# Two layers of adaptive-norm attention and feed-forward blocks on one core: exponentials straight from PSUM in the first attention, a PSUM bank of its own for the sums of squares in local attention, and empty places in the output stages

## The chip, the core and the metric

The kernel runs on one core of one Trainium2 chip, in one launch. The metric is the device time of one execution in microseconds (us). The engines are named as the profile names them: PE is TensorE (PEld its weight loads), DVE is VectorE, ACT is ScalarE, POOL is GpSimd and SP is SyncE, which issues the DMAs. Each engine works through its own instructions in order, and a semaphore holds an instruction back until what it needs is there.

## What is computed

The reference takes x of shape (2, 2048, 128) and runs two outer layers, all in float32. Cut to what matters:

```python
def layer(x, c, wmod, attention, model):
    sa, ca, ga, sb, cb, gb = modulation(c, wmod)       # per batch, 128 wide
    x = x + ga * attention(norm(x) * (1 + ca) + sa)
    x = x + gb * model(norm(x) * (1 + cb) + sb)
    return x

# L0 attention: 16 heads of 8; inside chunks of 64 positions a causal softmax,
#   across chunks a fast-weight state that is updated chunk by chunk (64 updates)
# L0 model: depth 6, 16 heads of 64, window 32;  L1 model: depth 2, 8 heads of 64, window 64
# L1 attention: causal linear attention (elu features) with its own feed-forward block

for l in range(depth):                                 # both models
    q, k, v = split(shift(x) @ Wqkv[l])
    q, k = rotary(l2norm(q) * qs, l2norm(k) * ks)      # l2norm: a root over 64 numbers
    p = softmax(mask(q @ k_window.T * 8))              # own and previous window
    x = x + (p @ v_window) @ Wo[l]
    a, g = split(layernorm(shift(x)) @ W1[l] + b1)
    x = x + (a * gelu(g)) @ W2[l] + b2
```

## The kernel before, in words

**First attention** (`l0_attention`). After the projections it walks over 32 tiles of 128 positions (`order`, `NT = 32`), under an order written out by hand (`manual_schedule`: every engine gets its instructions in the order in which the program makes them). Tile `i` passes through `spread` (POOL), `scores` (PE, into `ps_s`, two PSUM banks), `shifted` (DVE takes the row maximum of 16 groups of 64, line L430, and subtracts it, L432; ACT then makes one exponential over 1024 elements in SBUF, L433), `weights` (DVE sums, L438, and inverts, L439; POOL multiplies, L440), `keys_first` (PE transposes, L448; ACT copies out, L452), `values` (PE, L458; ACT copies to `vbd`, L465) and `mix` (64 small matmuls, L477; ACT copies to `hT`, L484). One turn of the loop works on four tiles at once: `keys_first(i)`, `weights(i+1)`, `scores(i+2)`, `values(i+1)`, `shifted(i+2)`, `mix(i)`.

Between these parts are seven places per tile, `slot(i, 0)` to `slot(i, 6)`, into which the items of the list `todo` are dealt out by the count `due`. Items 0 to 63 are `step(t)`: the 64 updates that form the products of transitions, four DVE instructions each (L374, L375, L377, L379). Item 64 writes them out (`products_done`). The other 65 items are the second part of the same attention: `transitions`, 32 `chain(n)` items, and `out_`, `centre`, `variance`, `scale` for each block of 512. `chain(n)` multiplies the running state by a transition (PE into `ps_n`, L560), adds the new write by a matmul with the identity (L565), copies the sum to SBUF (DVE, L571), and multiplies the old state with the output weights (PE, L575; ACT copies out, L580). The 64 updates are spread over the first 26 tiles, the rest over the last six.

**Local attention** (`local_models`). Eight layers (six of 16 heads, two of 8) of 32 tiles each make 256 rounds. Here a scheduler orders each engine's instructions by its own estimate of times, and picks which free buffer a PSUM tile gets. A round `i` holds, in the program: `scores(i+1)` (two PSUM banks from `psA`, L996 and L1005; DVE takes the maximum, L1013, and subtracts, L1015), ACT's exponential (L1022), DVE's sum (L1029) and inverse (L1030), POOL's product (L1031); `project(i+3, u)`, twice where there are 16 heads; `keys_first_(i)` (`ps_pT`, L1040; ACT copies, L1041); `mix(i)` (`ps_o`, L1058; ACT copies, L1064); `values(i+2)` (`ps_v`, L965; ACT copies, L966, and DMAs spread the rows); `turn(i+2)` (`ps_turn`, L946; ACT copies, L949 and L951) and `project_out(i)` (`ps_y`, L1075; DVE adds, L1081).

`project` is the part that the change touches. PE writes 1024 columns into a wide PSUM tile `ps_qk` (L879). ACT squares them (L881), DVE makes two products with the rotary table (L891, L896), POOL adds these (L902). After the last of the tile's projections DVE sums the squares of each head (L907) and takes a reciprocal root in nine small instructions (`rsqrt_quick`, L173 to L186), whose result `rq_y` POOL multiplies on (L914). The sums and the root's intermediate values lie in the last `ps_qk` itself:

```python
nc.vector.tensor_reduce(
    pq[:, 16 * v:16 * v + 16],
    st[i].pop(("sq", v)).rearrange("p (h d) -> p h d", d=DH), AX.X, ALU.add,
)
y = rsqrt_quick([pq[:, k * 32:k * 32 + 2 * H] for k in range(4)], 2 * H, wk)
```

The eight PSUM banks are shared out as `psA`, two wide tiles of two banks (`ps_qk`, `ps_s`), and `psT`, four single banks for all the others (`ps_pT`, `ps_o`, `ps_v`, `ps_turn`, `ps_y`, and `ps_c`, `ps_r`, `ps_f`, `ps_fy` of the feed-forward part).

The feed-forward part of a block of 512 positions is cut into seven items (`centre`, `variance`, `rest`, `scale`, `gate`, `up`, `down`) of which `step()` takes one at two places of each round. What follows a model (the linear attention after the first, `output` after the second) is cut in the same way, and `lstep()` takes one item at six places of each round. `output(b, k)` has three items: `fetch` loads a block of x, `residual` adds the model's result on DVE (L1205), `leave` transposes it on PE (L1449), copies it (ACT, L1453) and stores it. `rest` is an item that does nothing.

Of the kernel before, what the change touches and what calls it, by code (L numbers as in the profile page):

```python
# [72 lines left out]
def tile_kernel(ctx: ExitStack, tc: tile.TileContext, a: dict, out: bass.AP):  # L73
    nc = tc.nc
    DRAM = bass.MemoryType.DRAM
    PSUM = bass.MemoryType.PSUM
# [35 lines left out]
    identb = const.tile([128, 128], BF16, name="identb")  # L112
# [81 lines left out]
    def l0_attention():  # L194
# [18 lines left out]
        maskb = cp.tile([128, 8, 64], BF16, name="maskb")  # L213
# [8 lines left out]
        m, m1 = modulation()  # L222
# [185 lines left out]
        def scores(i):  # L408
            t0 = 128 * order[i]
            kx = L[i].pop("kx")  # L410
            sp = L[i]["s"] = psS.tile([128, 1024], F32, name="ps_s")
            for q in range(2):
                nc.tensor.matmul(
                    sp[:, 512 * q:512 * q + 512], lhsT=identb,
                    rhs=maskb.rearrange("p h k -> p (h k)"), start=True, stop=False,
                )
            for c in range(2):
                for q in range(2):
                    nc.tensor.matmul(
                        sp[64 * c:64 * c + 64, 512 * q:512 * q + 512],  # L420
                        lhsT=qT[64 * q:64 * q + 64, t0 + 64 * c:t0 + 64 * c + 64],
                        rhs=kx[64 * q:64 * q + 64, c].rearrange("p h j -> p (h j)"),
                        start=False, stop=True,
                    )

        def shifted(i):

            v = L[i].pop("s").rearrange("p (q h k) -> p h q k", q=2, h=8)
            mx = wk.tile([128, 8, 2], F32, name="mx")
            nc.vector.tensor_reduce(mx, v, AX.X, ALU.max)  # L430
            sm = L[i]["p"] = wk.tile([128, 8, 2, 64], F32, name="sm", bufs=3)
            nc.vector.tensor_tensor(sm, v, bc(mx.unsqueeze(3), (128, 8, 2, 64)), ALU.subtract)  # L432
            nc.scalar.activation(sm, sm, AF.Exp)  # L433

        def weights(i):
            sm = L[i]["p"]
            rs = wk.tile([128, 8, 2], F32, name="rs")
            nc.vector.tensor_reduce(rs, sm, AX.X, ALU.add)  # L438
            nc.vector.reciprocal(rs, rs)  # L439
            nc.gpsimd.tensor_tensor(sm, sm, bc(rs.unsqueeze(3), (128, 8, 2, 64)), ALU.mult)  # L440

# [109 lines left out]
        def chain(n):  # L551
            c = n % 8
            pm = E["p"][:, :, 128 * (n % 2):128 * (n % 2) + 128].rearrange(
                "p q (b f) -> p q b f", b=2)
            px = E["p"][:, :, 256:512].rearrange("p q (b f) -> p q b f", b=2)
            if n < 31:
                for b in range(B):
                    for q in range(2):
                        if n:
                            nc.tensor.matmul(  # L560
                                pm[QS[q], q, b], lhsT=E["bd"][QS[q], b, c],
                                rhs=E["m"][QS[q], b], start=True, stop=False,
                            )
                    for q in range(2):
                        nc.tensor.matmul(  # L565
                            pm[QS[q], q, b], lhsT=ident[QS[q], QS[q]],
                            rhs=E["rm"][QS[q], c % 2, b, c // 2], start=(n == 0), stop=True,
                        )
                mn = wk.tile([128, 2, 64], F32, name="mn")
                for q in range(2):  # L570
                    nc.vector.tensor_copy(mn[QS[q]], pm[QS[q], q])  # L571
            if n:
                for b in range(B):
                    for q in range(2):
                        nc.tensor.matmul(  # L575
                            px[QS[q], q, b], lhsT=E["m"][QS[q], b], rhs=wo10[QS[q], :],
                            start=True, stop=True,
                        )
# [93 lines left out]
        def slot(i, part):  # L672

            nonlocal done
            if i < 0:
                return
            q = 7 * i + part + 1
            due = 5 * q // 14 if i < 26 else 65 + (len(todo) - 65) * (q - 182) // 42
            while done < due:
                todo[done]()  # L680
                done += 1

        for i in range(-3, NT):
# [12 lines left out]
            slot(i, 2)  # L696
            if 0 <= i + 2 < NT:
                shifted(i + 2)
            slot(i, 3)
            if i >= 0:  # L700
                mix(i, 0)
                slot(i, 4)
                mix(i, 1)
            slot(i, 5)
            slot(i, 6)
            if i == -1:
                regroup()
# [8 lines left out]
    def local_models(mA, mB, hs0):  # L716
# [153 lines left out]
        def project(i, u):  # L870
            g, b, t = tiles[i]
            m, _ = layers[g]
            H, units = m.H, m.units
            tb = tabs[g, t]
            hw = hs[0][:, b, t * 128:(t + 1) * 128]
            pq = wide("qk")
            for j in range(2):
                js = slice(512 * j, 512 * j + 512)
                nc.tensor.matmul(pq[:, js], lhsT=hw, rhs=wts[g, u][:, js], start=True, stop=True)  # L879
            sq = wk.tile([128, 1024], F32, name="sq", bufs=2)  # L880
            nc.scalar.activation(sq, pq, AF.Square)  # L881
            r = wk.tile(
                [128, 1024], F32, tag=f"r{u if len(units) == 2 else i % 2}", name="r", bufs=2
            )
            t2 = wk.tile([128, 1024], F32, name="t2", bufs=1)
            same = units[u][0][0] == units[u][1][0]
            for e in range(1) if same else range(2):
                s = units[u][e][0]
                hn = 16 if same else 8
                es = slice(512 * e, 512 * e + 64 * hn)  # L890
                nc.vector.tensor_tensor(  # L891
                    r[:, es].rearrange("p (h d) -> p h d", d=DH),
                    pq[:, es].rearrange("p (h d) -> p h d", d=DH),
                    bc(tb[:, 0, s].unsqueeze(1), (128, hn, DH)), ALU.mult,
                )
                nc.vector.tensor_tensor(  # L896
                    t2[:, es].rearrange("p (h s d) -> p h s d", s=2, d=32),
                    pq[:, es].rearrange("p (h s d) -> p h s d", s=2, d=32)[:, :, ::-1, :],
                    bc(tb[:, 1, s].rearrange("p (s d) -> p s d", s=2).unsqueeze(1),
                       (128, hn, 2, 32)), ALU.mult,  # L900
                )
            nc.gpsimd.tensor_tensor(r, r, t2, ALU.add)  # L902
# [531 lines left out]
        def output(b, k):  # L1434
# [181 lines left out]
```

## Time and profile before

The time before is 4924.19 us, the median of three runs (4922.71 to 4925.23). The profiled execution took 4920.01 us; its span from the first to the last instruction is 4918.2 us, so 1.8 us lie around it.

| engine | busy us | share of the span | instructions |
|---|---|---|---|
| PE | 4474.6 | 91% | 73028 |
| PEld | 3055.6 | 62% | 73058 |
| DVE | 3946.2 | 80% | 6822 |
| ACT | 2635.7 | 54% | 4206 |
| POOL | 2780.6 | 57% | 1666 |

The shares are means over stages that are limited by different things, so the stages are read one by one. On the time axis of the span, the first part of the first attention with its 64 updates runs from 97 to 377 us, its second part with the chain to 546 us; local attention begins at 560 us, the linear attention is woven in around 3950 to 4350 us, and the blocks of the output leave between 4620 us and the end. In rows of the profile, "idle before" is the time for which an engine stood still ahead of an instruction, and the name behind `<-` is what ended that time. A busy PE is not a PE at its peak: matmuls are pipelined and their ends are modelled.

### The profile page before, as it was taken

The numbers are of one execution on the slowest core, as the hardware profiler recorded it, in microseconds if no ns is written. First come the engines' busy times: TensorE is split into PE (matmuls) and PEld (weight loads), VectorE is DVE, ScalarE is ACT, GpSimd is POOL, SyncE is SP. The second block draws the span as 40 slices with busy tenths as digits, with TensorE's granted clock in tenths as the row PEclk, the third lists the DMA queues.
The fourth block names the chain that finished last, engine by engine and source line by source line (L and its number), as shares of the span: only waits on it lengthen the run. The fifth ranks groups of instructions, "written<-read, shape, count | busy, mean of one in ns | idle before, by whom it ended". The sixth has DMA issues, their size and how long they took to land.

```text
span 4918.2 us, 166304 instructions
## 1 busy us (share of the span) xinstructions
PE 4474.6 (91%) x73028; PEld 3055.6 (62%) x73058; DVE 3946.2 (80%) x6822; ACT 2635.7 (54%) x4206; POOL 2780.6 (57%) x1666
## 2 busy tenths in 40 slices
PE   5657799999999999999999999999999998899997
PEld 4445566666666666666666666666666665556554
DVE  6993488888888888888887888888877777788886
ACT  3323355555555556555555555556555555465554
POOL 3332376666666666666665666666655544455552
PEclk8778899999999999999999999999999999999999
DMA  2000222222222322222222322222222111111121
GB/s 78 1 1 25 86 69 68 64 73 73 70 67 62 83 68 68 65 75 72 69 65 63 80 71 70 64 77 67 65 52 58 52 49 48 35 46 49 51 58 42
DMA packets 222467, 295.31 MB, mean 60 GB/s; under 512 B 75656, under 2 KB 95408, under 8 KB 221744
## 3 DMA queue, kind: packets, MB, share of 16 engines
q1 hardware_dynamic: 221744, 284.67, 22.0%
q8 instruction: 576, 9.44, 0.8%
q14 instruction: 147, 1.20, 0.1%
HBM read 40.98 MB, written 10.75 MB: 11 GB/s over the span
## 4 chain that ended last, share of the span: by engine, by line
PE 47%; DVE 26%; ACT 7%; POOL 5%; issue 4%; DMA 1%; SPq 0%; POOLq 0%; DVEq 0%; ACTq 0%
PE ps_qk L879 11%; PE ps_o L1058 5%; DVE ps_qk L907 5%; DVE t L896 5%; PE ps_f L1158 5%; PE ps_v L965 5%; PE ps_turn L946 4%; POOL r L902 4%; PE ps_y L1075 4%; DVE r L891 3%; PE ps_s L1005 3%; PE ps_fy L1183 3%; ACT sq L881 2%; DVE rs L1029 2%; PE ps_pT L1040 2%
## 5 line engine op out<-in xcount | busy, mean ns | idle before, releaser
L902 POOL TENSOR_TENSOR r<-r,t 128x1024 f32<-128x1024 f32 x448 | 1059.6, 2365 | 905.5 <-DVE t L896 800.1
L914 POOL TENSOR_TENSOR r<-r,rq_y 128x1024 f32<-128x1024 f32 x448 | 843.9, 1902 | 520.5 <-DVE rq_y L186 497.5
L881 ACT ACTIVATE sq<-ps_qk 128x1024 f32<-128x1024 f32 x448 | 460.4, 1028 | 1077.0 <-PE ps_qk L879 1010.5
L879 PE MATMUL ps_qk<-wp,hs 128*128 128x512 f32 x1792 | 885.7, 616 | 114.4 <-DVE rq_y L186 85.4
L891 DVE TENSOR_TENSOR r<-ps_qk,tb 128x1024 f32<-128x1024 f32 (+1 forms) x512 | 550.3, 1075 | 202.3 <-ACT sq L881 188.9
L896 DVE TENSOR_TENSOR t<-ps_qk,tb 128x1024 f32<-128x1024 f32 (+1 forms) x512 | 554.1, 1082 | 147.7 <-POOL r L902 147.1
L1058 PEld LDWEIGHTS ps_o<-pT,v 64*64 64x64 f32 (+1 forms) x26624 | 479.0, 135 | 304.7 <-ACT pT L1041 162.0
L1031 POOL TENSOR_TENSOR sm<-sm,rs 128x1024 f32<-128x1024 f32 x256 | 487.6, 1905 | 210.7 <-DVE rs L1030 124.3
L1058 PE MATMUL ps_o<-pT,v 64*64 64x32 f32 (+1 forms) x26624 | 529.7, 221 | 35.6 <-ACT pT L1041 18.9
L907 DVE TENSOR_REDUCE ps_qk<-sq 128x16 f32<-128x1024 f32 x448 | 549.0, 1225 | 11.9
L879 PEld LDWEIGHTS ps_qk<-wp,hs 128*128 128x128 f32 x1792 | 308.6, 192 | 370.4 <-issue 233.8
L946 PEld LDWEIGHTS ps_turn<-ident,r 128*128 128x128 f32 x3584 | 409.0, 142 | 125.9 <-issue 98.6
L965 PE MATMUL ps_v<-wp,hs 128*128 128x512 f32 x896 | 482.5, 639 | 1.5 <-ACT oT L1064 0.8
L1075 PEld LDWEIGHTS ps_y<-oT,wo 128*128 128x128 f32 x3584 | 430.3, 193 | 46.5 <-issue 42.4
L946 PE MATMUL ps_turn<-ident,r 128*128 128x128 f32 x3584 | 445.1, 276 | 11.2 <-POOL r L914 5.2
L1075 PE MATMUL ps_y<-oT,wo 128*128 128x128 f32 x3584 | 446.2, 277 | 1.5 <-ACT oT L1064 1.5
L1064 ACT COPY oT<-ps_o 128x512 f32<-128x512 f32 x448 | 243.4, 588 | 282.8 <-PE ps_o L1058 282.1
L1013 DVE TENSOR_REDUCE mx<-ps_s 128x16 f32<-128x1024 f32 (+1 forms) x256 | 312.5, 1221 | 95.9 <-PE ps_s L1005 94.1
L1005 PE MATMUL ps_s<-kT,qT 64*32 64x64 f32 (+1 forms) x26624 | 377.2, 230 | 0.1
L1005 PEld LDWEIGHTS ps_s<-kT,qT 64*32 64x32 f32 (+1 forms) x26624 | 325.6, 107 | 62.6 <-issue 51.7
L1158 PE MATMUL ps_f<-fx,w 128*128 128x512 f32 (+1 forms) x768 | 356.0, 600 | 2.5 <-DVE fx L1141 1.7
L1029 DVE TENSOR_REDUCE rs<-sm 128x16 f32<-128x1024 f32 (+1 forms) x256 | 310.5, 1213 | 51.1 <-ACT sm L1022 49.0
(265 smaller groups left out, 6833.2 us busy)
## 6 DMA issues: line engine op xcount, KB each, us to landing
v<-vn SPq DMA_DIRECT2D x1276, 128.0 KB
v<-vn SPq DMA_DIRECT2D x744, 64.0 KB
v<-vn SPq DMA_DIRECT2D x64, 256.0 KB
wp<-in_L_ffn_Wqkv SPq DMA_DIRECT2D x20, 512.0 KB
xD<-xb SPq DMA_DIRECT2D x24, 256.0 KB
xb<-xD SPq DMA_DIRECT2D x24, 256.0 KB
cs<-in_cos SPq DMA_DIRECT2D x128, 32.0 KB
cs<-in_sin SPq DMA_DIRECT2D x128, 32.0 KB
```

The lines of the kernel that those rows point to most:

```text
L879: nc.tensor.matmul(pq[:, js], lhsT=hw, rhs=wts[g, u][:, js], start=True, stop=True)
L891: nc.vector.tensor_tensor(r[:, es].rearrange("p (h d) -> p h d", d=DH), pq[:, es].rearrange("p (h d) -> p h d", d=DH), bc(tb[:, 0, s].unsq ...
L896: nc.vector.tensor_tensor(t2[:, es].rearrange("p (h s d) -> p h s d", s=2, d=32), pq[:, es].rearrange("p (h s d) -> p h s d", s=2, d=32)[: ...
L902: nc.gpsimd.tensor_tensor(r, r, t2, ALU.add)
L907: nc.vector.tensor_reduce(pq[:, 16 * v:16 * v + 16], st[i].pop(("sq", v)).rearrange("p (h d) -> p h d", d=DH), AX.X, ALU.add,)
L914: nc.gpsimd.tensor_tensor(rv, rv, bc(y[:, 16 * v:16 * v + 16].unsqueeze(2), (128, 16, DH)), ALU.mult)
L946: nc.tensor.transpose(p[:, c * 128:(c + 1) * 128], r[:, cs], ident)
L965: nc.tensor.matmul(p, lhsT=hw, rhs=wv, start=True, stop=True)
L1005: nc.tensor.matmul(sp[W * w:W * w + W, c0:c0 + 2 * W], lhsT=qT[64 * q:64 * q + 64, cc, W * w:W * w + W], rhs=kT[64 * q:64 * q + 64, cc, W ...
L1058: nc.tensor.matmul(po[s][64 * q:64 * q + 64, 128 * c + W * w:128 * c + W * w + W], lhsT=v2[kp, w, co:co + 64], rhs=pT[kp, q, c, W * w:W * ...
L1075: nc.tensor.matmul(py[:, 0:128], lhsT=wts[g, "o"][:, c * NO + s, :], rhs=oT[:, s, c, :], start=(c + s == 0), stop=(c == 3 and s == NO - 1),)
L1158: nc.tensor.matmul(ps_[c][0:sz], lhsT=wts[g, "w1"][:, o:o + sz], rhs=S["x"], start=True, stop=True,)
```

## The change

Four things change.

1. First attention, softmax: scores of the two groups of heads go to two PSUM tiles of one bank each, `ps_s0` and `ps_s1`, in that order. DVE takes the negated maxima of each half (two reductions of 512 instead of one of 1024) and no longer subtracts. ACT makes 16 exponentials of 64 columns straight from PSUM, with the negated maximum as bias; the eight of the first half also give their sums (`accum_out`). DVE sums only the other half. The eight exponentials of the second half come after `mix(i, 1)`.
2. First attention, chain and dealing: the matmuls with the identity go; DVE adds the new write where it copied. The 64 updates are dealt out over 28 tiles instead of 26, the other items over four tiles instead of six.
3. Local attention: `psT` has three banks instead of four, and a new pool `psR` of one bank holds the sums of squares and the root's intermediate values, which no longer lie in `ps_qk`.
4. Output: `rest` stands between `fetch` and `residual`, and between `residual` and `leave`.

```diff
         def scores(i):
...
-            sp = L[i]["s"] = psS.tile([128, 1024], F32, name="ps_s")
             for q in range(2):
+                sp = L[i]["s", q] = psS.tile([128, 8, 64], F32, name=f"ps_s{q}")
+                flat = sp.rearrange("p h k -> p (h k)")
                 nc.tensor.matmul(
...
-        def shifted(i):
-
-            v = L[i].pop("s").rearrange("p (q h k) -> p h q k", q=2, h=8)
-            mx = wk.tile([128, 8, 2], F32, name="mx")
-            nc.vector.tensor_reduce(mx, v, AX.X, ALU.max)
-            sm = L[i]["p"] = wk.tile([128, 8, 2, 64], F32, name="sm", bufs=3)
-            nc.vector.tensor_tensor(sm, v, bc(mx.unsqueeze(3), (128, 8, 2, 64)), ALU.subtract)
-            nc.scalar.activation(sm, sm, AF.Exp)
+        def maxima(i):
+            mx = L[i]["mx"] = wk.tile([128, 8, 2], F32, name="mx")
+            for q in range(2):
+                nc.vector.tensor_reduce(mx[:, :, q], L[i]["s", q], AX.X, ALU.max, negate=True)
+
+        def exps(i, q):
+            if q == 0:
+                L[i]["p"] = wk.tile([128, 8, 2, 64], F32, name="sm", bufs=3)
+                L[i]["rs"] = wk.tile([128, 8, 2], F32, name="rs")
+            sp, mx = L[i].pop(("s", q)), L[i]["mx"]
+            for h in range(8):
+                nc.scalar.activation(
+                    L[i]["p"][:, h, q, :], sp[:, h, :], AF.Exp, bias=mx[:, h, q:q + 1],
+                    accum_out=L[i]["rs"][:, h, q:q + 1] if q == 0 else None,
+                )
 
         def weights(i):
-            sm = L[i]["p"]
-            rs = wk.tile([128, 8, 2], F32, name="rs")
-            nc.vector.tensor_reduce(rs, sm, AX.X, ALU.add)
+            sm, rs = L[i]["p"], L[i].pop("rs")
+            nc.vector.tensor_reduce(rs[:, :, 1], sm[:, :, 1, :], AX.X, ALU.add)
             nc.vector.reciprocal(rs, rs)
...
                                 pm[QS[q], q, b], lhsT=E["bd"][QS[q], b, c],
-                                rhs=E["m"][QS[q], b], start=True, stop=False,
+                                rhs=E["m"][QS[q], b], start=True, stop=True,
                             )
-                    for q in range(2):
-                        nc.tensor.matmul(
-                            pm[QS[q], q, b], lhsT=ident[QS[q], QS[q]],
-                            rhs=E["rm"][QS[q], c % 2, b, c // 2], start=(n == 0), stop=True,
-                        )
                 mn = wk.tile([128, 2, 64], F32, name="mn")
                 for q in range(2):
-                    nc.vector.tensor_copy(mn[QS[q]], pm[QS[q], q])
+                    r = E["rm"][QS[q], c % 2, :, c // 2]
+                    if n:
+                        nc.vector.tensor_tensor(mn[QS[q]], pm[QS[q], q], r, ALU.add)
+                    else:
+                        nc.vector.tensor_copy(mn[QS[q]], r)
...
-            due = 5 * q // 14 if i < 26 else 65 + (len(todo) - 65) * (q - 182) // 42
+            due = 65 * q // 196 if i < 28 else 65 + (len(todo) - 65) * (q - 196) // 28
...
             if 0 <= i + 2 < NT:
-                shifted(i + 2)
+                maxima(i + 2)
+                exps(i + 2, 0)
             slot(i, 3)
             if i >= 0:
                 mix(i, 0)
                 slot(i, 4)
                 mix(i, 1)
+            if 0 <= i + 2 < NT:
+                exps(i + 2, 1)
...
-        psT = ctx2.enter_context(tc.tile_pool(name="f_psT", bufs=4, space=PSUM))
+        psT = ctx2.enter_context(tc.tile_pool(name="f_psT", bufs=3, space=PSUM))
+        psR = ctx2.enter_context(tc.tile_pool(name="f_psR", bufs=1, space=PSUM))
...
+                ss = psR.tile([128, 128], F32, name="ps_ss")
                 for v in range(len(units)):
                     nc.vector.tensor_reduce(
-                        pq[:, 16 * v:16 * v + 16],
+                        ss[:, 16 * v:16 * v + 16],
...
-                y = rsqrt_quick([pq[:, k * 32:k * 32 + 2 * H] for k in range(4)], 2 * H, wk)
+                y = rsqrt_quick([ss[:, k * 32:k * 32 + 2 * H] for k in range(4)], 2 * H, wk)
...
-            return fetch, residual, leave
+            return fetch, rest, residual, rest, leave
```

More of the change, by code (lines that the diff above doesn't have):

```diff
@@ L410, in scores @@
             kx = L[i].pop("kx")
-            sp = L[i]["s"] = psS.tile([128, 1024], F32, name="ps_s")
             for q in range(2):
+                sp = L[i]["s", q] = psS.tile([128, 8, 64], F32, name=f"ps_s{q}")
+                flat = sp.rearrange("p h k -> p (h k)")
                 nc.tensor.matmul(
-                    sp[:, 512 * q:512 * q + 512], lhsT=identb,
-                    rhs=maskb.rearrange("p h k -> p (h k)"), start=True, stop=False,
-                )
-            for c in range(2):
-                for q in range(2):
+                    flat, lhsT=identb, rhs=maskb.rearrange("p h k -> p (h k)"),
+                    start=True, stop=False,
+                )
+                for c in range(2):
                     nc.tensor.matmul(
-                        sp[64 * c:64 * c + 64, 512 * q:512 * q + 512],
+                        flat[64 * c:64 * c + 64, :],
                         lhsT=qT[64 * q:64 * q + 64, t0 + 64 * c:t0 + 64 * c + 64],
@@ L561, in chain @@
                                 pm[QS[q], q, b], lhsT=E["bd"][QS[q], b, c],
-                                rhs=E["m"][QS[q], b], start=True, stop=False,
+                                rhs=E["m"][QS[q], b], start=True, stop=True,
                             )
-                    for q in range(2):
-                        nc.tensor.matmul(
-                            pm[QS[q], q, b], lhsT=ident[QS[q], QS[q]],
-                            rhs=E["rm"][QS[q], c % 2, b, c // 2], start=(n == 0), stop=True,
-                        )
                 mn = wk.tile([128, 2, 64], F32, name="mn")
                 for q in range(2):
-                    nc.vector.tensor_copy(mn[QS[q]], pm[QS[q], q])
+                    r = E["rm"][QS[q], c % 2, :, c // 2]
[3 more added lines that the diff above has]
+                        nc.vector.tensor_copy(mn[QS[q]], r)
             if n:
```

## The prediction

> **What bounds the kernel now.** I cut the span into stages first (windows; columns: stretch, then length, busy us and instructions of PE, PEld, DVE, ACT, POOL, then granted clock, DMA share, GB/s).
>
> ```profile
> 97.00:377.00 280.00, 171.84 (x2306) 117.64 (x2332) 269.86 (x358) 86.19 (x200) 98.31 (x53) 0.76 0.00 1
> 377.00:546.00 169.00, 129.13 (x1729) 101.20 (x1733) 52.70 (x114) 56.44 (x126) 29.38 (x22) 0.85 0.08 25
> 560.00:3950.00 3390.00, 3235.22 (x60713) 2225.04 (x60713) 2801.94 (x4574) 1922.68 (x3018) 2144.97 (x1260) 0.99 0.27 69
> 4600.00:4890.00 290.00, 257.88 (x2324) 167.82 (x2323) 236.29 (x475) 156.01 (x237) 137.25 (x82) 0.96 0.18 51
> ```
>
> DVE fills 96% of the first stage, PE 76% of the second, PE 95% of the six wide layers, PE 89% where the output leaves. So DVE's work counts in the first stage, and PE's idle time everywhere else. What PE waits for (waits on PE; total us, times, longest):
>
> ```profile
> PE ps_qk L879 <- DVE rq_y L186: 85.4, 83, 3.6
> PE ps_n L575 <- DVE mn L571: 29.5, 30, 2.3
> PE ps_o L1058 <- ACT pT L1041: 18.9, 59, 2.0
> PE ps_out L1449 <- DVE xb L1205: 14.7, 3, 5.1
> PE ps_out L1449 <- issue: 11.3, 4, 4.9
> ```
>
> The first row is the wait that the new bank removes: PE may not overwrite `ps_qk` until the root's last instruction has read it. One ordinary round (timeline, PE and DVE) shows how the wait closes a loop, and what else is near it:
>
> ```profile
> 677.93 1.99 PE L879 MATMUL ps_qk<-wp,hs 128*128 128x512 f32 x4 [0.80 <-DVE rq_y L186]
> 681.01 1.23 DVE L891 TENSOR_TENSOR r<-ps_qk,tb 128x1024 f32<-128x1024 f32 x1 [0.74 <-ACT sq L881]
> 682.45 0.37 PE L1058 MATMUL ps_o<-pT,v 64*64 64x32 f32 x4
> 682.75 1.12 PE L965 MATMUL ps_v<-wp,hs 128*128 128x512 f32 x2
> 687.04 1.23 DVE L896 TENSOR_TENSOR t<-ps_qk,tb 128x1024 f32<-128x1024 f32 x1 [1.31 <-POOL r L902]
> 692.92 0.19 DVE L186 SCALAR_TENSOR_TENSOR rq_y<-ps_qk,rq_g 128x32 f32<-128x32 f32 x1
> ```
>
> The period of 15.2 us is that loop: PE's own round is 14.4, DVE's without the 0.74 is 14.5. And `ps_v` stands between the first and the other `ps_o`: it fills the time until ACT's second copy of `ps_pT` (ends 682.88).
>
> Two tenths of a percent, 9.8 us, is about what a measurement here can tell from no change. I sum against the profiled execution, 4920.0 us, which is 4.2 below the median of the three runs; the result goes onto the median.
>
> **First attention, updates.** Before, 26 tiles take 280 us, 10.77 each: 64 updates of 0.66+0.70+0.69+0.76 = 2.80 make 179, the tile's 1.22+1.22+1.21+0.25 = 3.90 make 101. After, the halves cost what the 128x512 reductions cost (0.695): 2.34 a tile, 28 tiles 66, sum 245 us. But that sum is no longer the bound, because DVE must now wait: the sums of the next turn need the eight late exponentials, those stand on ACT behind `hT`, which stands behind the eight early ones, which need the maxima. Price of an exponential: no row shows 64 columns with a bias. Copies of 128x170 and 128x512 (305, 581 ns) give 0.81 ns a column, so 219 ns; a biased 128x512 (L1168, 685) is 99 above a copy (586); two copies in a row overlap by 110 (pair 1.06). So 208 ns apart, 3.4 us for 16. Price of giving out a sum: not shown; between nothing and 0.2 us (the smallest ACT row, 128x4, is 205 ns); I take that row less the overlap, 0.1, 0.8 us a tile. The loop: 3.4 + 0.8 + `hT` 0.53 + sums and inverse 0.87 + the one update that falls between (2.8) + maxima 1.36 + hand-overs 0.2 = 9.96; a third of the turns has two updates in the other part, where DVE sets 10.6. Mean 10.2, 28 tiles 285: **+5 us**. With nothing for the sums 270 (-10); with 0.2 for each and the overlap kept the loop is 10.76, 301 (+21); with 0.2 and half the overlap 11.64, 326 (+46). Behind the waiting sums on DVE stand the updates, and behind these ACT's copies of their products (L383): none of it is needed before item 64.
>
> [...]
>
> **First attention, chain.** Two of six tiles leave the 169 us: 64 `mix` matmuls 2.1, transposes 1.1, scores 1.9, values 0.45, 5.5 of PE each, -11. The identity matmuls: 31 times some 0.4, -12. DVE's add costs what its copy did (64x128 rows L1081 and L571: 0.29 both). Against it: chain items stand closer, so ACT's copies L580 (two of 0.37) are waited for more often, +6; four tiles' exponentials keep ACT 3.1 longer each, in part in front of these copies, +4. **-13 us**, between -24 and +5. First attention: **-8**.
>
> **Local attention, the gain.** With sums and root in their own bank `ps_qk` is free when L896 has read it, 4 us sooner. PE's 85.4 us go, but the next is late too. In rounds without feed-forward work at that place, the second projection then meets DVE's subtraction (rounds without the first wait show that wait, 0.34), or `mix` meets ACT's copies. Following a group of eight rounds (1119 to 1235 us, waits 0.88, 0.56, 0.79, 0.21), 1.3 of 2.44 us stay; of 24 such groups 31 us. Six groups begin with waits near 3.4 and 2 us, because DVE waits for POOL's table; there PE's matmuls after the wait run slowly (3.68 for 1.98), and some 3 us more are saved, 20 in all; the first rounds add 4. Gain **55** of the 85 us.
>
> **Local attention, the price.** Three banks serve what four served; at each place one more copy must be out. In the built order `ps_v` stands after all 64 `ps_o`, since it waits for a bank: PE idles until the second copy of `ps_pT`. Over the trace `ps_v` fills 13 us before these copies end in the 85 rounds where this is the place; a group of eight rounds has about three of them, and some of it lies in the wait that the gain already counts: 0.35 a group. `ps_y` waits for the second `ps_turn` copy, 0.1 in four rounds: 0.4. `up` ahead of `ps_pT`: both transposes share a bank and `mix` waits for the second of DVE's three products: 0.6. `gate` ahead of `ps_y` waits for the first gelu behind a table load of 1.28: 0.5. The round with both: 0.2. Together 2.05, in 24 groups **49 us**. The later `ps_v` starts the DMAs of its rows on SP some 3 us later; `mix` reads them two rounds, 30 us, on: nothing. The eight narrow layers' rounds: the order puts the projection between `ps_pT` and `mix`, which hides 0.24 in two of three rounds (-10); six more table loads of 1.28 and the same waits take that back. Net **-6**, between -40 and +35.
>
> [...]
>
> **Output.** The two rows are 26.0 us; the last 4.7 is the end's and stays. After each of the three waits near 5 us the next stretch of PE is slow (eight `ps_c` 1.92 for 1.06): 7 more. Of 28, with a place (1.8 us) more on each side of the DVE sum, I take **-20** (10 to 28); the DMA (3 us) and DVE's 1.5 then pass beside other work. On SP no load moves ahead of another. The tail's items run with nothing between them: nothing.
>
> **Sum.** -8 -6 -20 = -34: 4886 on the profiled execution, **4890 us** on the median.
>
> **Rivals.** *Three banks bound PE* (slower). ACT's copies stand one behind the other after `mix`; if they come 0.3 us later than I read, each of 256 rounds pays 0.3 at `ps_turn` or `ps_y`: +77 us, 4967. It decides from 0.13 us a round (34/256). For: ACT waits for `ps_o` itself in 207 rounds, so nothing is ahead but each copy follows tightly; against: it is in time to 0.1. *ACT bounds the updates*: 0.2 us for each sum and half the overlap, +46 instead of +5: 4890+41 = 4931. For: 16 instructions in the loop; against: ACT was busy 31% of the stage. *Everything is gained*: no wait takes the place of 85.4, and the groups' prices vanish in DVE's freed time: 4890-30-49 = 4811. For: DVE has 17% to spare in the wide layers. *The empty places do nothing*, since six places in a round are passed without PE coming there: 4910.
>
> **How the numbers follow.** My forecast 0.50, banks 0.14, ACT 0.15, everything 0.13, empty places 0.08. The forecast's own terms spread some 25 us each way (4865 to 4915). The range, 4835 to 4945, takes these in, with the empty places and most of the case of ACT, and leaves out most of the banks and most of everything, 0.2 in all. Faster than 4914.3: 0.44 of the forecast, everything 0.13, empty places 0.05: 0.62. Within 0.2%: 0.05 of the forecast, 0.07 of ACT, 0.03 of the empty places: 0.15. Slower: the rest, 0.23.
>
> **What would show it.** Right: no wait of L879 on L186; waits of L879 on L1015 and of L1058 on L1041 above 30 us; L1075 with waits on L951 and L1168; first stage 275 to 295 us; no wait of 5 us at L1449. Wrong: exponentials above 0.3 us apart; PE's share of the wide layers under 95%; `ps_turn` waiting for its own copies.

## The result, and the profile after

The changed kernel takes 4946.39 us (median of four executions, 4939.28 to 4953.25) beside 4923.45 of the kernel before: ratio 1.0047, 95% interval 1.0033 to 1.0061. It is 23 us slower. The forecast was 4890 with a range of 4835 to 4945: wrong in sign, and just outside the range.

The windows of the profiled execution of the changed kernel (span 4947.8 us), the same four stretches as before, with the same columns:

```profile
97.00:377.00 280.00, 219.58 (x2528) 135.22 (x2524) 234.73 (x371) 184.06 (x867) 107.91 (x59) 0.79 0.01 2
377.00:546.00 169.00, 131.70 (x1194) 98.53 (x1193) 37.42 (x94) 48.48 (x141) 18.84 (x16) 0.65 0.08 24
560.00:3950.00 3390.00, 3263.78 (x60059) 2225.95 (x60059) 2758.27 (x4509) 1907.57 (x2983) 2121.08 (x1247) 0.99 0.27 69
4600.00:4890.00 290.00, 271.00 (x2539) 173.92 (x2538) 248.73 (x527) 178.08 (x265) 156.83 (x94) 0.98 0.20 55
```

Three things stand in it. In the updates DVE falls from 270 to 235 us, as meant, and PE rises from 172 to 220. In the chain PE has 535 matmul records fewer in the 169 us (a float32 matmul leaves two records here, as the 124 identity matmuls are 248 records of L565 before; the identity matmuls and two tiles are gone from the stretch, and the chain is not at its end at 546 us) and is busy all the same, at a granted clock of 0.65 where it was 0.85. In the wide layers PE is busier by 29 us and gets 654 matmul records fewer done. What PE waits for now:

```profile
PE ps_o L1070 <- issue: 48.8, 41, 1.8
PE ps_n L582 <- DVE mn L576: 30.8, 30, 2.9
PE ps_o L1070 <- ACT pT L1053: 29.6, 23, 3.5
PE ps_qk L890 <- DVE sm L1027: 25.8, 25, 3.4
PE ps_out L1461 <- DVE xb L1217: 5.1, 2, 4.5
```

The wait of `ps_qk` for the root (85.4 us) is gone, and of the output's 26.0 us some 6 are left (5.1, and 0.8 put down to issue). The waits were removed, and the time rose.

Every execution has its own mean granted clock, and a kernel's times differ by it. Over 90 executions of the kernel before, on five chips, they go from 4909.5 to 4938.6 us at clocks of 0.965 to 0.958, and a line through them falls by 24 us for each 0.01 of the clock (correlation -0.69). One execution says little about 10 us, so the verdicts below rest on ratios of several.

### The profile page after: what moved, and what is told of

It reads as the page before. It is cut to its first block, busy times and chain, and to the rows that moved or that the text cites. A ratio compares the mean times of both kernels' runs of the same rounds, so it can differ in the third digit from the quotient of the medians.

```text
span 4947.8 us, 166703 instructions
## 1 busy us (share of the span) xinstructions
PE 4602.9 (93%) x72810; PEld 3097.6 (63%) x72810; DVE 3871.3 (78%) x6822; ACT 2748.9 (56%) x4948; POOL 2779.7 (56%) x1666
## 4 chain that ended last, share of the span: by engine, by line
PE 60%; DVE 12%; ACT 11%; issue 4%; POOL 2%; DMA 0%; SPq 0%; POOLq 0%; ACTq 0%; DVEq 0%
PE ps_qk L890 11%; PE ps_o L1070 9%; PE ps_v L977 8%; PE ps_y L1087 7%; PE ps_turn L958 7%; PE ps_s L1017 5%; PE ps_f L1170 3%; PE ps_fy L1195 3%; ACT sm L1034 2%; PE ps_pT L1052 2%; ACT sq L892 2%; DVE t L907 2%; ACT pT L1053 2%; DVE ps_ss L919 1%; POOL r L913 1%
## 5 line engine op out<-in xcount | busy, mean ns | idle before, releaser
L1070 PEld LDWEIGHTS ps_o<-pT,v 64*64 64x64 f32 (+1 forms) x26624 | 498.1, 135 | 282.7 <-ACT pT L1053 177.5
L1070 PE MATMUL ps_o<-pT,v 64*64 64x32 f32 (+1 forms) x26624 | 545.5, 221 | 86.0 <-issue 48.8
L919 DVE TENSOR_REDUCE ps_ss<-sq 128x16 f32<-128x1024 f32 x448 | 545.9, 1219 | 4.6
L958 PE MATMUL ps_turn<-ident,r 128*128 128x128 f32 x3584 | 465.5, 278 | 15.9 <-POOL r L926 7.5
L1087 PE MATMUL ps_y<-oT,wo 128*128 128x128 f32 x3584 | 456.3, 279 | 4.1 <-ACT oT L1076 1.5
```

The costliest lines, as they stand in the source:

```text
L919: nc.vector.tensor_reduce(ss[:, 16 * v:16 * v + 16], st[i].pop(("sq", v)).rearrange("p (h d) -> p h d", d=DH), AX.X, ALU.add,)
L958: nc.tensor.transpose(p[:, c * 128:(c + 1) * 128], r[:, cs], ident)
L1070: nc.tensor.matmul(po[s][64 * q:64 * q + 64, 128 * c + W * w:128 * c + W * w + W], lhsT=v2[kp, w, co:co + 64], rhs=pT[kp, q, c, W * w:W * ...
L1087: nc.tensor.matmul(py[:, 0:128], lhsT=wts[g, "o"][:, c * NO + s, :], rhs=oT[:, s, c, :], start=(c + s == 0), stop=(c == 3 and s == NO - 1),)
```

## Experiments: the parts one by one

Each of these is the kernel before with one part of the change.

**Parts 1 and 2** (exponentials, chain, dealing).

> Parts 1 and 2 of the change alone (first attention: exponentials from PSUM, no identity matmuls, dealing over 28 tiles). My theory, from the two traces: the updates come 9 us sooner (last L379 at 367.2 for 375.9 us), but in the chain PE runs at half its clock for 123 us instead of 55, because it has less to do between its waits, and the stage ends 12 us later: 4935 (4928 to 4942). Rival, the forecast's own sum of -8 with the loss elsewhere: 4915.

Measured: 4952.81 (4947.77 to 4955.43), ratio 1.0052 (1.0038 to 1.0066), 25 us slower than before. My theory after the traces said 12: the sign is right, the size doubled. Its 9 us for the updates compare the 64th and last update of the one trace with the 63rd of the other; like for like the last L379 ends 4.7 us sooner (371.9 for 376.6).

**Part 3** (three banks, and one for the root).

> Part 3 alone (three banks and one for the root). My theory: the new bank takes away the 85 us of L879 waiting for L186, but three banks make PE wait elsewhere; from the end of the first attention to the last exponential of the 30th tile of the last layer the changed kernel lost some 30 us, so 4953 (4943 to 4963). Rival A, the forecast: -6, 4917. Rival B, only the phase of the rounds against the shifted start costs, not the banks: within 5 us of 4923.

Measured: 4939.90 (4924.74 to 4958.54), ratio 1.0024 (1.0012 to 1.0037): 12 us slower, short of my 30 and outside both rivals.

**Part 4** (empty places).

> Part 4 alone (empty places in the output). From the two traces the end gains some 14 us: 4909 (4901 to 4914), as the waits of 5 us at L1449 go. Rival: the end's gain came from the three banks' other order, and the places do nothing: 4923.

Measured: 4920.26 (4908.70 to 4931.34), ratio 0.9983 (0.9972 to 0.9994): 8 us faster. Waits on PE in its profile, from 4500 us on:

```profile
PE ps_out L1449 <- DVE xb L1205: 8.3, 4, 4.6
PE ps_out L1449 <- issue: 3.1, 2, 2.8
```

Of 26.0 us 11.4 are left. Of the three waits near 5 us one is nearly gone (0.6) and two became 2.8, since the sum L1205 still takes up to 2.94 us.

25 + 12 - 8 = 29, beside 23 (16 to 30) for the whole: the parts add up within their intervals.

## Experiments: what the bank is worth

Gain and price of part 3 can be separated.

```diff
-        psT = ctx2.enter_context(tc.tile_pool(name="f_psT", bufs=4, space=PSUM))
+        psT = ctx2.enter_context(tc.tile_pool(name="f_psT", bufs=3, space=PSUM))
```

> Three banks for the small tiles, but the sums and the root stay in the projection's own tile (one bank is left unused): the price of the bank without the gain. Part 3 as a whole cost 12 us. Theory G (a real gain and a larger price, as the forecast had it): 30 to 70 us slower than before, 4955 to 4995. Rival N (the wait of L879 for L186 stands where PE would wait anyway, so its removal brings nothing and the banks cost the 12): 4935 to 4945.

Measured: 5003.44 (4991.28 to 5023.13), ratio 1.0174 (1.0151 to 1.0197). By the ratio one bank less costs 86 us. With the root in that bank it is 12, so the removal of the wait is worth 74 (56 to 91 by the two intervals): theory G, a real gain eaten by a larger price, here larger than its 30 to 70. The price shows only in part as idle time. Groups on PE in the wide layers, first of the kernel with part 4 alone (whose local attention before the output is that of before), then with three banks; columns: busy, mean ns, then idle before:

```profile
L1058 PE MATMUL ps_o<-pT,v 64*64 64x32 f32 x24464 | 436.4, 221 | 21.9 <-issue 15.9 <-ACT pT L1041 5.7
L946 PE MATMUL ps_turn<-ident,r 128*128 128x128 f32 x3064 | 369.6, 274 | 7.2 <-ACT oT L1064 3.2 <-DVE am L1326 2.2 <-POOL r L914 1.9
```

```profile
L1058 PE MATMUL ps_o<-pT,v 64*64 64x32 f32 x24448 | 454.0, 220 | 46.0 <-issue 31.7 <-ACT pT L1041 5.8
L946 PE MATMUL ps_turn<-ident,r 128*128 128x128 f32 x3056 | 387.1, 276 | 7.2 <-POOL r L914 3.6 <-DVE ps_qk L173 3.1 <-ACT vn L966 0.2
```

`ps_turn` is "busy" for 17.5 us more and `ps_o` for 17.6 more, with nearly the same number of matmuls of the same mean length, besides 24 more of idle ahead of `ps_o`. The matmuls of a row overlap in the trace (3056 of 276 ns would be 843 us end to end, and the group is busy for 387), so a short delay between two of them takes from the overlap and counts as busy; only the growth of the group against its mean duration tells it.

Can the gain be had without the price? Two other places for the sums:

```diff
+                ss = wk.tile([128, 128], F32, name="rs2")     # SBUF; cs: bufs=1
...
-                        pq[:, 16 * v:16 * v + 16],
+                        ss[:, 16 * v:16 * v + 16],
```

> Part 3 in another way: four banks stay, and the sums and the root's values lie in SBUF (for which the small tile of rotary tables has one buffer instead of two). Takes away the same wait without the price of a bank. My theory, that the banks are what cost: faster than before by the forecast's gain without its price, 55 us, 4868 (4850 to 4890). Rival A: what is late next (DVE, ACT's copies) takes nearly all of the 85 us whatever the banks: 4915 to 4930. Rival B: the single buffer of tables or DVE's small instructions in SBUF cost it: above 4930.

Measured: 4979.27 (4970.41 to 4981.94), ratio 1.0100 (1.0085 to 1.0115): 50 us slower, rival B. The root's instructions on DVE in the wide layers, the first as it was before, then three here:

```profile
L173 DVE TENSOR_SCALAR ps_qk<-ps_qk 128x32 f32<-128x32 f32 x192 | 38.0, 198 | 5.2
```

```profile
L173 DVE TENSOR_SCALAR rs<-rs 128x32 f32<-128x32 f32 x188 | 147.8, 786 | 5.0
L175 DVE TENSOR_SCALAR rq_g<-rs 128x32 int32<-128x32 int32 x188 | 49.8, 265 | 4.5
L182 DVE SCALAR_TENSOR_TENSOR rs<-rs,rq_h 128x32 f32<-128x32 f32 x188 | 36.0, 192 | 6.4
```

In PSUM L173 took 198 ns. The single buffer of tables was not tried apart. I first put the longer instruction down to the form with one operand and a constant:

```diff
-        nc.vector.tensor_scalar(xm, x, 1e-24, None, ALU.max)
+        nc.vector.scalar_tensor_tensor(xm, x, 1e-24, x, ALU.max, ALU.max)
```

(and likewise the next one, with the constant in a tile).

> Sums and root in SBUF with four banks, as in the run that was 50 us slower, where the two instructions with one operand and a constant (L173, L175) took 786 and 265 ns in the wide layers and 939 and 745 in the narrow ones; here both are written with two operand tiles, like the others, which stayed near 190 ns there. Theory: these two were the whole loss in the narrow layers (50 us there), so narrow layers as before; in the wide layers the wait is gone without a bank's price: theory G 4880 to 4905, rival N 4920 to 4930. Should they still take over 700 ns, it is not their form, and the time stays near 4975.

Measured: 4971.62 (4970.52 to 4977.82), ratio 1.0106 (1.0092 to 1.0120); the rewritten instruction takes 790 ns in the wide layers. My theory fell. The timeline of this run, DVE and POOL, shows what the instruction ends with:

```profile
1040.38 2.37 POOL L925 TENSOR_TENSOR r<-r,t 128x1024 f32<-128x1024 f32 x1 [0.82 <-DVE t L919]
1041.40 1.40 DVE L194 SCALAR_TENSOR_TENSOR rs<-rs 128x32 f32<-128x32 f32 x1
1042.83 0.19 DVE L196 SCALAR_TENSOR_TENSOR rq_g<-rs,seed 128x32 int32<-128x32 int32 x1
```

DVE's small instruction ends with POOL's big one (1042.80 and 1042.75). In the 240 of its 256 cases in which it began while POOL worked it ended 0.05 us after POOL (mean); in PSUM the same step took its 0.19 us (mean of 174 cases) though it began while POOL worked. Both forms of the instruction end with POOL's (the first 0.03 us behind it in the mean), and last 786 and 790 ns in the wide layers, so the form is not the cause; what ties the two engines together no run shows. So in this kernel the root's values are better off in PSUM, which is where the kernel before has them.

```diff
+                ss = bank("ss")                               # one of the four psT banks
```

> The sums and the root in a tile of the shared pool of four banks: a bank is away for the root only while it is worked on (about 5 of 15 us). Theory G: the gain stays, the price is a third: faster than before, 4890 to 4915. Rival N: the removal brings nothing and a third of the price stays: 4927 to 4935.

Measured: 5740.04 (5735.21 to 5741.53), ratio 1.1663 (1.1647 to 1.1679): both theories fell. Its waits on PE:

```profile
PE ps_turn L947 <- DVE rq_y L186: 316.5, 119, 5.6
PE ps_s L997 <- DVE t L896: 180.0, 108, 2.4
PE ps_y L1076 <- DVE rq_y L186: 65.2, 17, 4.6
```

The wait on the root moved to the next tiles of the pool: `ps_turn`, `ps_y` and others now stand behind it, for more than the 85 us of before. The tile is held through two sums and nine small instructions, where the pool's other tiles are emptied by a copy or two.

## Experiments: what happens in the first attention

Parts 1 and 2 cost most, so I took them apart as well.

> Part 2 without its dealing: only the identity matmuls go and DVE adds the new write; everything else as before. Parts 1 and 2 together cost 24 us. Theory C (clock): it is the chain's PE that has too little to do between its waits and falls to half clock; then taking matmuls away brings nothing or costs: 4929 to 4940 beside 4927 of before, and over 75 us of half clock between the last update and the end of the first attention. Rival (the forecast): 12 us of PE work gone, 4915. Rival S: the loss comes from the exponentials and the dealing alone, so this is 4915 to 4927.

Measured: 4929.98 (4921.42 to 4938.52), ratio 1.0007 (0.9997 to 1.0018). Taking 124 matmuls (248 records) out of the chain brings nothing.

> Part 1 with the dealing over 28 tiles, identity matmuls kept as before. Theory C: less than the 24 us of both parts together, 4930 to 4940, since PE keeps the matmuls that hold its clock. Rival S: all of the loss, 4946 to 4955, because ACT's exponentials and the separated score matmuls stand in the way of the chain.

Measured: 4944.03 (4931.34 to 4952.65), ratio 1.0034 (1.0022 to 1.0046), 17 us. Between the theories: most of the loss comes with the exponentials and the dealing, which were not tried apart.

> Parts 1 and 2 as in the change, but with the score matmuls in the old order: both mask matmuls first, then four score matmuls in a row, in the four quarters of the array. In the changed order they were busy 85 us, in the old 48. If that is a part of the 24 us: 4940 beside 4951. Rival: in the updates DVE and ACT bound the stage and PE has room, in the chain only four tiles are left: 4948 to 4953. Against it: the exponentials of the first half then wait for all of the scores, up to 4958.

The edit, in `scores`:

```diff
-                for c in range(2):
+            for c in range(2):
+                for q in range(2):
                     nc.tensor.matmul(
```

Measured: 4934.01 (4931.51 to 4943.40), ratio 1.0021 (1.0013 to 1.0030), 10 to 15 us less than with the changed order, whose ratio was 1.0052 above and 1.0042 in a second measurement below. I had not seen this at all: in the diff the loops only change places. Score matmuls in the first attention, of the kernel before, of the changed one and of this one:

```profile
L419 PE MATMUL ps_s<-kx,qT 64*64 64x512 f32 x256 | 48.3, 835 | 9.1 <-issue 3.5 <-POOL kx L401 3.2
```

```profile
L419 PE MATMUL ps_s<-kx,qT 64*64 64x512 f32 x256 | 85.2, 748 | 2.9 <-POOL kx L401 2.9
```

```profile
L420 PE MATMUL ps_s<-kx,qT 64*64 64x512 f32 x256 | 50.3, 867 | 2.9 <-POOL kx L401 2.9
```

The records of four 64x64 matmuls in a row, in four quarters of the array, overlap: 256 of 835 ns in 48.3 us are 4.4 at a time. With a mask matmul over the whole array after every two it is 2.2 (256 of 748 ns in 85.2 us).

Does PE lose its clock because it has less to do (theory C)? Useless matmuls in each chain step:

```diff
+                for b in range(B):
+                    for q in range(2):
+                        nc.tensor.matmul(pd[QS[q], q, b], lhsT=ident[QS[q], QS[q]],
+                            rhs=E["rm"][QS[q], c % 2, b, c // 2], start=True, stop=True)
```

> Parts 1 and 2 as in the change, and four matmuls with the identity in each chain step whose result nobody reads (they write the columns that the next step overwrites). They add 12 us of PE work at the old place. Theory C: the chain stage gets no longer, or shorter, than without them: 4940 to 4950 beside 4951, half clock in it under 100 us instead of 127. Rival (PE's work is what counts): 8 to 12 us longer, 4960.

Measured: 4936.33 (4921.14 to 4951.75), ratio 1.0018 (1.0007 to 1.0029), 16 us faster than without them. But the profiled execution, whose span of 4949.7 us lies at the upper end of these times, shows a longer chain at a low clock (213.9 us, 162.0 of them at half clock, where theory C asked for under 100; without the useless matmuls 200.4 and 128.5). So both side by side on one chip:

> Parts 1 and 2 of the change once more, now on the same chip and in the same rounds as the next one. If the 25 us of the first measurement hold: ratio 1.004 to 1.0065 to the kernel before.

> The same with four useless matmuls with the identity in each chain step, beside it on one chip. Theory C (they hold PE's clock): again 10 us or more faster than without them, ratio 1.001 to 1.003. Rival (the first difference came from the chips or from the luck of a few runs, and 124 matmuls cost their time): equal to the run without them or up to 10 us slower, ratio 1.005 to 1.007.

Measured: without 4949.57 (4940.51 to 4953.83), ratio 1.0042 (1.0030 to 1.0054); with 4939.03 (4929.87 to 4953.18), ratio 1.0028 (1.0015 to 1.0041). Twice the useless work cost nothing, and the clock of the executions was higher with it (0.9575 to 0.9555 in the mean, both times); a gain of 7 to 16 us is likely, but the intervals of the second pair overlap. The profiled chain was again longer with them (210.9 us to 204.8), so the gain does not lie there. From the last L622 to the end, where all these kernels have the program of before, the two profiled executions without them took 4371.9 and 4374.7 us, the two with them 4362.6 and 4361.8, and five of other kernels with that program 4357.3 to 4368.9 (the kernel before, the chain's edit alone, the exponentials with the dealing, the scores in the old order, and the split chain below). So the pair does not bear theory C out, and some 10 of the 25 us that parts 1 and 2 cost lie behind the first attention in their two profiled executions; why, no run shows.

Then I looked for the waits themselves. L575 (output products) waits 30 times, 29.5 us, for L571, DVE's copy of other columns of the same two banks:

```diff
-            E["p"] = pool.tile([128, 2, 512], F32, name="ps_n")
+            E["p"] = [pool.tile([128, 512], F32, name=f"ps_n{k}") for k in "mx"]
...
-                for q in range(2):
-                    nc.vector.tensor_copy(mn[QS[q]], pm[QS[q], q])
+                nc.vector.tensor_copy(mn, pm)
```

> Kernel before, only the chain changed: the new state's products go to one PSUM bank and the output products to another (before, the two halves of each lay in both), so that L575 need not wait for DVE's copy L571, and one copy of 128 partitions takes the place of two of 64 on DVE and on ACT. Theory: the 30 waits of 29 us in all go, and PE, with shorter gaps, keeps its clock longer: the chain is 25 to 40 us shorter, 4885 to 4900. Rival: the next step needs DVE's copy anyway, so only the shorter copies count, some 10 us: 4915.

Measured: 4859.22 (4858.14 to 4867.51), ratio 0.9878 (0.9865 to 0.9892): 60 us faster than before, more than I expected. The edit takes away the wait, halves the number of copies, lets the output products alternate between two ranges of columns and changes the clock; the four were not tried apart. The wait is gone, and the clock of the chain is 0.93 (from the end of the last update but one to the start of the last L622):

```profile
L575 PE MATMUL ps_nx<-wo,mn 64*64 64x128 f32 x248 | 19.9, 281 | 4.4 <-ACT bx L579 4.4
```

```profile
372.10:507.10 135.00, 121.56 (x1798) 96.30 (x1801) 51.89 (x97) 48.66 (x102) 31.45 (x25) 0.93 0.16 46
```

Four kernels on top of it:

> Kernel before with the split chain (62 us faster alone) and the empty places of the output (8 faster alone). If the two add up: 4853 (4846 to 4860). Rival: the output's waits depend on the phase in which the blocks arrive, and 8 us are not kept: 4860 to 4866.

> The whole change, with the chain split over two banks. Theory C: the first attention of the change lost its 24 us because its chain's PE, waiting 30 times for DVE's sums and with fewer matmuls, ran at half clock; without these waits that loss goes, and with the new order's 12 us for the banks and 8 back for the places the time is near 4865 (4855 to 4875). Rival S: the loss is in ACT's exponentials and stays: 4885 to 4895.

> As the whole change with the split chain, and with the score matmuls in the old order besides, four in a row in the four quarters of the array (15 us with the old chain). If that order costs by what PE does in the updates: 10 to 15 us faster than without it. If it cost only because PE's work in the updates set the clock at the chain's start: within 5 us.

> As the kernel before with split chain and empty places, and without the identity matmuls (DVE adds in its one instruction). With the waits gone theory C says that PE keeps its clock without them, so the 12 us of PE work that the forecast counted now come: 4840 to 4848 beside 4853. Rival: the chain is now a sequence of latencies, in which 0.2 us a step go: 4846 to 4853.

| kernel | median us | ratio to before (95%) |
|---|---|---|
| before, split chain, empty places | 4852.50 | 0.9858 (0.9839 to 0.9877) |
| the same without identity matmuls | 4869.27 | 0.9884 (0.9868 to 0.9900) |
| whole change, split chain | 4886.20 | 0.9914 (0.9895 to 0.9933) |
| the same, scores in the old order | 4885.40 | 0.9913 (0.9896 to 0.9930) |

Split chain and places add up (expected 4853). The whole change gains 65 us by the split chain but stays 28 behind the first row, of which 12 are the bank's. That is the time of rival S, but not its place: in the profiled executions the first attention of the whole change ends only 4 us later than that of the first row (506.2 to 502.2 us), and the rest is 33 us longer. The order of the scores is worth nothing here; why it was worth 10 to 15 with the old chain stays open. And without the identity matmuls the kernel is 13 us slower, not faster (the intervals overlap slightly); DVE's add takes the 0.29 us that its copy took, so it is not the rival's 0.2 us a step. Windows of the chain, from the end of the last update but one to the start of the last L622, of the first two rows of the table, in that order:

```profile
371.50:502.20 130.70, 117.81 (x1802) 92.50 (x1801) 51.99 (x98) 48.53 (x102) 31.53 (x25) 0.97 0.16 46
```

```profile
372.10:511.40 139.30, 125.37 (x1554) 96.55 (x1553) 52.24 (x98) 48.59 (x102) 31.42 (x24) 0.85 0.14 38
```

248 matmul records fewer, and PE is busy for 7.6 us more, at a clock of 0.85 for 0.97. Theory C, as it stood ahead of this run, said that PE would keep its clock here; it did not. What the pair does show, with one profiled execution on each side, is that matmuls taken out can cost more clock than they save work.

## Why the prediction was wrong

**Updates: the terms held.** An exponential of 64 columns follows the one before in 0.199 us in the mean (forecast 0.208), a pair of exponential and sum in 0.292, so the sum adds 0.09 (forecast 0.1). The timeline of the changed kernel, ACT:

```profile
240.29 0.31 ACT L439 ACTIVATE sm<-ps_s,mx 128x64 f32<-128x64 f32 x1 [0.82 <-DVE mx L429]
240.50 0.19 ACT L439 ACTIVATION_READ_ACCUMULATOR sm<-ps_s,mx 128x1 f32 x1
240.60 0.31 ACT L439 ACTIVATE sm<-ps_s,mx 128x64 f32<-128x64 f32 x1
...
243.49 1.75 ACT L439 ACTIVATE sm<-ps_s,mx 128x64 f32<-128x64 f32 x8
```

The sum is an instruction of its own, 0.19 to 0.24 us long, more than half of it overlapped. The tiles came 9.8 us apart instead of the forecast's 10.2, and the last update ended at 371.9 us, where it was 376.6 before. The forecast's +5 was -5 by these two profiles, and -4 to -7 beside six other executions with the first attention of before (375.8 to 378.6): an error to the good side. The rival in which ACT bounds the updates is out.

**Chain: the step that failed.** Beside the forecast's -8, -6 and -20 the first attention, the bank and the places measured +25, +12 and -8, so the first attention was furthest off, and in it the chain's -13. "The identity matmuls: 31 times some 0.4, -12" and "Two of six tiles leave the 169 us ... -11" count PE's work at a fixed clock and take all of it off the time. The chain's clock was not fixed. The trace's record of the granted clock has only 1.0 and 0.5, nearly always in stretches of a multiple of 3.41 us (113 of 114 records of the kernel before, 119 of 120 of the changed one). What sets the one or the other no run shows; the longest wait of PE in the chain of before was 2.25 us, and the clock fell to half eight times there. Profiled executions, from the end of the last L379 to the start of the last L622:

| kernel | chain us | of it at half clock |
|---|---|---|
| chain of before: before | 181.0 | 51.5 |
| the same: part 3 alone, part 4 alone | 189.8, 187.9 | 80.6, 75.3 |
| the same: root in SBUF, three banks, shared pool, root in SBUF with rewritten form | 184.2, 185.6, 186.0, 192.0 | 61.5, 69.6, 66.6, 82.8 |
| without identity matmuls | 182.6 | 76.8 |
| identity matmuls kept, exponentials and dealing new | 198.4 | 112.6 |
| parts 1 and 2; a second execution | 200.4; 204.8 | 128.5; 150.2 |
| whole change | 197.9 | 122.9 |

The first three rows are one and the same program in this stretch. Over its seven executions the length goes with the time at half clock, 0.33 us for each us (correlation 0.98; mean length 186.7), and the profile of before that I read was the shortest of them. The chain of parts 1 and 2 was 14 to 18 us longer than the mean, where the forecast had it 13 shorter. The windows of the first row and of parts 1 and 2:

```profile
376.60:557.60 181.00, 138.39 (x1789) 108.10 (x1789) 56.41 (x123) 58.38 (x130) 30.39 (x24) 0.86 0.10 30
```

```profile
373.60:574.00 200.40, 154.27 (x1370) 117.09 (x1371) 44.89 (x114) 60.31 (x170) 22.91 (x20) 0.68 0.10 28
```

PE has 419 matmul records fewer, and it is busy for 16 us more and idle for 3.5 more. The line through the seven, drawn on to 128.5 and 150.2 us of half clock, would give the old chain 206 and 213 us, 5 to 8 more than measured. So as an estimate, far beyond the 82.8 us to which the line reaches, the work that left is worth 5 to 8 us at an equal clock, and the clock takes more than that. Another estimate goes by the mean clocks of whole executions (0.9556 to 0.9609, at 24 us for 0.01): 13 of the 24 us that separate the medians. Why the clock fell is open. That matmuls taken out lower it is shown in the split chain alone, by one pair of executions. In the old chain the same edit left the half clock within the spread of the seven (76.8 us), and useless matmuls put in did not bring it back. Most of its growth comes with the new exponentials and the dealing (112.6 us with the identity matmuls kept), which were not tried apart.

**Scores: a step that was missing.** I costed `scores` at nothing, and the new order made it busy for 85 us instead of 48.

**Local attention: both sizes too small, the price more.** The forecast had a gain of 55 and a price of 49, and the mechanism of both. The runs say 74 and 86. In the wide layers `ps_o` pays 42 us (growth and idle) where I had 28 (0.35 + 0.6 + 0.2 in 24 groups), `ps_turn` 17.5 where I had nothing, and `ps_y` 9 (6.6 and 2.1) where I had 22 (0.4 + 0.5). The first rival named the mechanism, "`ps_turn` waiting for its own copies", at 77 us more than my sum; the net was +12 where I had -6.

**Output: oversized.** 8 us (3 to 14) for the forecast's 20. The three waits near 5 us were to go whole; two became 2.8, since the sum L1205, 0.75 us alone, still takes up to 2.94 where one of POOL's products of 2.34 us begins beside it.

**Chances.** The sign was given to faster with 0.62 because the first attention's and the output's terms were taken as nearly certain, and no rival had PE's clock in it, though the view of windows showed 0.85 in the chain and 0.99 in the wide layers.

## What to carry to other kernels

Read the granted clock of a stage, over several executions, before costing its matmuls: with the split chain, 248 matmul records fewer came with a clock of 0.85 for 0.97 (one pair of executions), and taking out 29.5 us of waits came with 60 us less time. A PSUM bank is a resource like an engine's time: measure its price by leaving it empty (86 us here), and look for it in busy time that grows at an equal mean (17.5 and 17.6 us here). When two traces are compared, count the instances of a line, so that the last of one is not set beside the last but one of the other. Where an instruction waits for another one that uses different columns of the same bank, move the columns; here the edit of ten lines that did so gave 60 us; with the empty places the kernel is at 4852.50, faster than both.

## What was not expected of the hardware

- One and the same chain program took 181.0 to 192.0 us in seven executions, and its length went with its time at half clock, 51.5 to 82.8 us; in the shortest of them the clock fell to half eight times, and PE's longest wait was 2.25 us.
- A mask matmul over the whole array between 64x64 matmuls in different quarters takes half of their overlap away: 48.3 to 85.2 us for 256 records.
- A 128x32 instruction of DVE in SBUF takes 0.19 us or up to 2.3, ending with POOL's instruction (0.05 us behind it in the mean of 240 cases); with its values in PSUM it took 0.19 us while POOL worked (mean of 174 cases).
